# A two-layer decoder on one core: scores in halves of keys, scaling a step later, and a router with fewer steps in its context attention

## The chip, the core and the metric

The kernel runs on one core of a Trainium2 chip. A core has five engines that take their instructions from queues of their own: TensorE (PE in the profile, its weight loads apart as PEld), VectorE (DVE), ScalarE (ACT), GpSimd (POOL) and SyncE (SP, which here only starts DMAs). The metric is the device time of one execution in microseconds (us); where a time stands alone it is the median of several executions. All data are 32-bit floats.

## What is computed

The program is a decoder of two layers over 8 batches of 512 tokens with 256 features, with a context of 64 rows per batch. Each layer has a self-attention, an attention with the context and a feed-forward part, and a layer norm follows every part. The change touches the second layer's attention with the context and what prepares its experts. Of the reference these lines matter:

```python
def _L1_xattn_ref(x1, x2, Wq1, Wk1, Wv1, Wk2, Wv2, Wo, bo):
    ...
    q1 = split_heads(x1 @ Wq1, N1)
    k1 = split_heads(x1 @ Wk1, N1)
    v1 = split_heads(x1 @ Wv1, N1)
    k2 = split_heads(x2 @ Wk2, N2)
    v2 = split_heads(x2 @ Wv2, N2)
    k = jnp.concatenate([k1, k2], axis=1)
    v = jnp.concatenate([v1, v2], axis=1)
    sim = jnp.einsum('bihd,bjhd->bhij', q1.astype(jnp.float32), k.astype(jnp.float32)) * scale
    attn = jax.nn.softmax(sim, axis=-1)
    out = jnp.einsum('bhij,bjhd->bihd', attn, v)
    out = out.reshape(B, N1, h * d)
    return out @ Wo + bo

def _L1_ffn_ref(x, gamma, beta, router_w, W1, W2):
    ...
    xn = (x - mu) * jax.lax.rsqrt(var + EPS) * gamma + beta
    logits = jnp.einsum('btd,ed->bte', xn, router_w)
    probs = jax.nn.softmax(logits / TEMP, axis=-1)
    w, idx = jax.lax.top_k(probs, K)
    wdense = jnp.sum(jax.nn.one_hot(idx, E, dtype=w.dtype) * w[..., None], axis=-2)
    h = jax.nn.silu(jnp.einsum('btd,edf->betf', xn, W1))
    y = jnp.einsum('betf,efd->betd', h, W2)
    out = jnp.einsum('bte,betd->btd', wdense, y)
    return out + res
```

There are 8 heads of 64 and 8 experts. So a softmax runs over 576 keys (512 of the tokens, 64 of the context), and the experts' part needs, for every token, the two experts with the greatest weights. The kernel computes only those two: it sorts the tokens by expert in a table in memory.

## The kernel before

**Stages.** The program runs six stages one after the other: layer 0's self-attention, its context attention and feed-forward part, layer 1's self-attention, layer 1's context attention (about 2175 to 3031 us in the trace), the experts (to about 3558 us), and the last norm. The change lies in the fourth stage, with its ends reaching into the fifth.

**The pipeline of the context stage.** `_pipeline` (L32) walks over units and, in each step, calls a list of stages, each with a lag. The units are batch b (8), pair of heads c (4) and query tile i (4 tiles of 128 tokens): 128 steps. In each step stand, in this order (L1491 ff.): `l1x_scores` of this unit, `l1x_transposes` of the unit two steps ago, `l1x_values` of the unit six steps ago, and `l1x_ahead`. At the end of each step one piece of a list `put_off` is taken and run. In this stage PE executes strictly the written order (`tc.manual_schedule(engines={PE})`); the other engines' instructions are ordered by a scheduler when the program is built, except where `keep_in_program_order` stands.

- `l1x_scores`: for each of the two heads j, one matmul over the 512 token keys (L1100) and one over the 64 context keys (L1102) into a tile `s_sc` of two PSUM banks; then DVE takes the negated maximum `nm` (L1104), ACT the exponential with the sum beside it (L1105), and `scaled` (L898) the reciprocal of the sums (`rsum`, L900) and the scaling of p by it (L902). The context keys `k2` are computed once ahead of the stage. A head's 64 rows of q and k lie in partitions 0 to 63 or 64 to 127.
- `l1x_transposes`: one transposition of the middle 128 columns of p, which hold the context part of both heads (`tP2`, L1115), and four for each head (`tP`, L1120); each is copied out of PSUM by `evac` (L104), which gives every other copy to DVE (L108) and the rest to ACT (L110).
- `l1x_values`: o is summed over key tiles (L1132), and with the last tile the context's values are added (L1140). Then `out_done` (L961) follows: o is copied into `aT`, and after the fourth pair of heads the two halves of the output projection (`project_and_norm`, L239) are put on `put_off`. The second half ends in `normed`, the layer norm (DVE `bn_stats` and `bn_aggr`, POOL's power for the inverse root L216, DVE's x at L223).
- `l1x_ahead`: in step i=0 the q projection of the next pair of heads, in i=2 its k, in i=3 its v (L1057, L1067); k's result is copied to SBUF by DVE (L1062). In i=1 the transposition of the next batch's x (`tT`, L198) or its context values, in some pairs.

**Banks.** PSUM has two score tiles of two banks (s), three transposition tiles of one bank (t), and one o tile. With one o tile `u_tile` (L98) gives t tiles too, so the projections (`t_qk`, `t_v`), the output projection and the router all share the three t banks with `tP` and `tP2`.

**The router's pieces.** `routed` (L1472) puts behind each batch's output projection: nothing, `route_norm`, nothing, `route_transposes`, nothing, `route_picks`, nothing, `route_places`, one for each step. So one batch's router runs beside the next batch's attention. `route_norm` (L1180) makes z, a row tile with one buffer, and stores 2x as the start of the sum `total`. `route_transposes` turns z (`tZ`, L1198). `route_picks` (L1208) makes the logits (`o_r`, L1213), the softmax over 8 experts, the two picks, and writes weights and token numbers into z (L1243, L1244). `route_places` (L1247) counts with 14 small matmuls (`o_rank`, L1252 to L1256) how many tokens have taken each expert ahead of each token, works out the rows, and POOL scatters z's rows into the table `rows_in` with eight indirect DMAs (L1268). The first few lines of the counting:

```python
for i in range(NT):
    pe.matmul(o[:, i * NE : (i + 1) * NE], lhsT=under, rhs=both[:, i, :], start=True, stop=(i == 0))
    for j in range(i):
        pe.matmul(o[:, i * NE : (i + 1) * NE], lhsT=ones, rhs=both[:, j, :], start=False, stop=(j == i - 1))
```

**To the experts.** For batch 6, `routed` also puts `early_blocks` (which expert and which rows each of the first blocks of 256 rows takes) and the load of the first block on `put_off`. Batch 7's router pieces go on `last_route` and run beside the first blocks of the expert stage. A block goes through `moe_load` (L1383: SP loads the rows xr, then the two weights, `we`), a step with nothing, `moe_pre` (transposes, L1403), `moe_up` (L1425) and `moe_down` (L1433). `moe_down` computes both token tiles of a block in one bank `o_y` (L1442), DVE scales each (L1462), and POOL adds each to `total` with an indirect DMA (L1463). The last stage loads `total`, takes the norm and stores it.

Of the kernel before, what the change touches and what calls it, by code (L numbers as in the profile page):

```python
# [11 lines left out]
F32 = mybir.dt.float32  # L12
# [6 lines left out]
P = 128  # L19
# [30 lines left out]
def decoder_kernel(ctx: ExitStack, tc: tile.TileContext, a: dict, out: bass.AP):  # L50
# [967 lines left out]
    NC2 = NB * S2  # L1018
    k2 = slot("k2").rearrange("p (c n) -> p c n", c=4)
# [28 lines left out]
    def l1x_project(b, c, what):  # L1048

        xT = live["xT", b]  # L1050
        cols = slice(c * P, (c + 1) * P)
        if what == 0:
            live["qk", b, c] = qk_tiles()
        if what < 2:
            t = t_tile("t_qk").rearrange("p i n -> p (i n)")
            for kc in range(KC):
                pe.matmul(t, lhsT=(wq1, wk1)[what][:, kc, cols], rhs=xT[:, kc, :], start=(kc == 0), stop=(kc == KC - 1))  # L1057
            if what == 0:

                act.mul(live["qk", b, c][0], t, 0.125)  # L1060
            else:
                dve.tensor_copy(live["qk", b, c][1], t)  # L1062
            return
        t = t_tile("t_v")
        for j in range(NT):
            for kc in range(KC):
                pe.matmul(  # L1067
                    t[:, j, :],
                    lhsT=xT[:, kc, j * P : (j + 1) * P],
                    rhs=wv1[:, kc, cols],  # L1070
                    start=(kc == 0),
                    stop=(kc == KC - 1),
                )
        v = ph.tile([P, NT, P], F32, tag="vc", name="vc", bufs=3)
        act.copy(v, t)
        live["qkv", b, c] = *live.pop(("qk", b, c)), v
# [13 lines left out]
    def l1x_scores(b, c, i):  # L1090
        q, k, _ = live["qkv", b, c]
        p = p_tile(S + S2, bufs=4)
        sums = col("sums", 4)
        nm = col("nm", 2)
        for j in range(2):
            h = 64 * j
            lhsT = q[h : h + 64, i * P : (i + 1) * P]
            s = s_tile("s_sc").rearrange("p t n -> p (t n)")

            pe.matmul(s[:, S * j : S * (j + 1)], lhsT=lhsT, rhs=k[h : h + 64, :], start=True, stop=True)  # L1100
            at = S - S2 * j
            pe.matmul(s[:, at : at + S2], lhsT=lhsT, rhs=k2[h : h + 64, c, b * S2 : (b + 1) * S2], start=True, stop=True)  # L1102
            s = s[:, at * j : at * j + S + S2]
            dve.tensor_reduce(nm[:, j : j + 1], s, AX.X, ALU.max, negate=True)  # L1104
            act.activation(p[:, j, :], s, AF.Exp, bias=nm[:, j : j + 1], accum_out=sums[:, j : j + 1])  # L1105
        scaled(p, sums, S + S2)
        live["p", b, c, i] = p

    def l1x_transposes(b, c, i):
        p = live.pop(("p", b, c, i)).rearrange("p j n -> p (j n)")  # L1110
# [5 lines left out]
        evac(pt2[:, i * P : (i + 1) * P], t)  # L1116
        for j in range(2):
# [3 lines left out]
            evac(pt[j][:, :, i * P : (i + 1) * P], t)  # L1121
# [86 lines left out]
    def route_picks(b):  # L1208
# [11 lines left out]
        pr, top, hit, rest = e_tile("pr"), e_col("top"), e_tile("hit"), e_tile("rest")  # L1220
# [5 lines left out]
        dve.tensor_tensor(pr, pr, over_e(top), ALU.mult)  # L1226

        left = pr
        picks = []
        for k in range(2):  # L1230
            pick = e_tile(f"pick{k}")
            dve.tensor_reduce(top, left, AX.X, ALU.max)
            dve.tensor_tensor(hit, left, over_e(top), ALU.is_equal)
            dve.tensor_tensor(hit, hit, over_i(rev), ALU.mult)
            dve.tensor_reduce(top, hit, AX.X, ALU.max)
            dve.tensor_tensor(pick, over_i(rev), over_e(top), ALU.is_equal)
            if k == 0:
                dve.scalar_tensor_tensor(rest, pick, -2.0, pr, ALU.mult, ALU.add)
                left = rest
            picks.append(pick)  # L1240
        both, z = e_tile("both"), live["z", b]
# [3 lines left out]
        live["picks", b] = picks, both  # L1245

    def route_places(b):  # L1247

        picks, both = live.pop(("picks", b))
        o = u_tile("o_rank")  # L1250
        for i in range(NT):
            pe.matmul(o[:, i * NE : (i + 1) * NE], lhsT=under, rhs=both[:, i, :], start=True, stop=(i == 0))  # L1252
            for j in range(i):
                pe.matmul(o[:, i * NE : (i + 1) * NE], lhsT=ones, rhs=both[:, j, :], start=False, stop=(j == i - 1))
        for i in range(NT):
            pe.matmul(o[:, NT * NE : (NT + 1) * NE], lhsT=ones, rhs=both[:, i, :], start=(i == 0), stop=(i == NT - 1))  # L1256
# [178 lines left out]
    def moe_down(n):  # L1435
# [3 lines left out]
        o = u_tile("o_y").rearrange("p (i n) -> p i n", i=TILES)  # L1439
        for i in range(size):  # L1440
            for f in range(8):
                pe.matmul(  # L1442
                    o[:, i, :],
# [17 lines left out]
        for i in range(size):  # L1461
            dve.tensor_scalar(y[:, i, :], o[:, i, :], share[:, i : i + 1], None, ALU.mult)  # L1462
# [11 lines left out]
    def routed(b):  # L1474
        pieces = [partial(f, b) for f in (route_norm, route_transposes, route_picks, route_places)]
# [5 lines left out]
        for piece in pieces:  # L1481
            put_off.extend((nothing, piece))
# [4 lines left out]
    with phase("l1_context") as ph, tc.manual_schedule(engines={PE}):  # L1487
        l1x_share(0)
        l1x_context_values(0)
        for what in range(3):  # L1490
# [3 lines left out]
            [(0, l1x_scores), (2, l1x_transposes), (6, l1x_values), (0, l1x_ahead)],  # L1494
# [111 lines left out]
```

## Time and profile before

| | us |
|---|---|
| median of 3 runs (lowest, highest) | 3592.87 (3590.85, 3603.25) |
| the profiled execution: its time | 3602.03 |
| its span in the trace | 3600.3 |
| context stage of layer 1, 2175 to 3031: PE, DVE, ACT, POOL busy | 796.3, 537.0, 335.9, 83.4 of 856 |
| expert stage, 3031 to 3558: PE, DVE, ACT, POOL busy | 519.8, 67.0, 120.5, 117.0 of 527 |

The profile is one execution, recorded by the hardware; its granted TensorE clock was 0.961 over the span. In the listing of instructions each line has start, duration, engine, line of the kernel, operation, output and input by their names with partitions and columns (`64*128 64x512` is a weight of 64 rows and 128 columns against 64 rows and 512 columns), and how many of them are joined (`x4`; a matmul of 32-bit data shows as two, its two passes, and a transposition as one); in brackets the time that the engine stood idle before, and what released it. In the list of waits the numbers are total us, times, longest us; the first name waits, the second released it. In the table by stretch the columns are the length, busy us of PE, PEld, DVE, ACT and POOL with their instruction counts, the granted clock, the share of DMA and GB/s.

### The profile page before, as it was taken

The page shows a single profiled execution, that of the slowest core. Times are in us where ns is not written, and L with a number is a line of the kernel's source. Part 1 is how long each engine was busy: PE and PEld are TensorE (multiplying, and loading weights), DVE is VectorE, ACT ScalarE, POOL GpSimd, SP SyncE. Part 2 cuts the span into 40 slices and gives each one's busy share as a digit, 9 for nine tenths or more (in the row PEclk, how much of TensorE's full clock was granted, in tenths as well). Part 3 has the DMA queues.
Part 4 walks back from the last instruction along what each step waited for, and adds up shares of the span by engine and source line. Part 5 has one row for each costly group of instructions (what it writes and reads, how often), then busy time and mean ns, then how long its engine had stood idle before and what let it go on. Part 6 is the DMA issues. An engine that isn't in the chain of part 4 may idle for free. (4 is left out here: it accounts for less than half of the span.)

```text
span 3600.3 us, 52648 instructions
## 1 busy us (share of the span) xinstructions
PE 3374.1 (94%) x19718; PEld 2124.2 (59%) x19718; DVE 2080.9 (58%) x5710; ACT 1504.2 (42%) x3139; POOL 1097.2 (30%) x960
## 2 busy tenths in 40 slices
PE   8999999998999989999999999999999998999995
PEld 3333343345666656666666665555555555888884
DVE  5776766665666467777777766665666664201012
ACT  2444444443443345565555654433433333222222
POOL 3877777771111122222222210010110111222222
PEclk8999999997999999999999999999999998999997
DMA  4001011111000099332322320000000003666674
GB/s 133 31 16 32 18 34 38 34 46 32 5 2 1 1 233 255 42 42 36 40 38 36 42 42 4 10 19 16 19 14 14 19 13 125 207 189 184 185 230 133
DMA packets 166000, 234.96 MB, mean 65 GB/s; under 512 B 26569, under 2 KB 128649, under 8 KB 165746
## 3 DMA queue, kind: packets, MB, share of 16 engines
q1 hardware_dynamic: 139010, 175.83, 15.7%
q0 software_dynamic: 25584, 51.57, 9.6%
q8 instruction: 156, 2.56, 0.3%
q10 hardware_dynamic: 1152, 4.19, 0.3%
q14 instruction: 98, 0.80, 0.1%
HBM read 135.83 MB, written 61.11 MB: 55 GB/s over the span
## 5 line engine op out<-in xcount | busy, mean ns | idle before, releaser
L428 DVE CUSTOM_DVE_ANT_0 scored<-s_sc,decay 128x512 f32<-128x512 f32 x512 | 323.5, 687 | 220.5 <-PE s_sc L423 219.4
L281 ACT ACTIVATE p<-p,nm 128x128 f32<-128x128 f32 (+3 forms) x512 | 282.5, 553 | 301.3 <-DVE nm L270 300.0
L865 POOL DMA_DIRECT2D qk<-turned x256 | 207.9, 1228 | 592.5 <-issue 303.8
L481 ACT ACTIVATE pt<-s_st 128x1024 f32<-128x1024 f32 x256 | 261.1, 1023 | 272.0 <-PE s_st L477 240.3
L1105 ACT ACTIVATE p<-s_sc,nm 128x576 f32<-128x576 f32 x256 | 191.1, 747 | 342.5 <-DVE nm L1104 241.9
L902 DVE TENSOR_SCALAR p<-p,rsum 128x576 f32<-128x576 f32 (+4 forms) x768 | 300.1, 432 | 9.8
L1425 PE MATMUL s_h<-xnT,we 128*128 128x256 f32 (+1 forms) x1248 | 261.6, 363 | 1.5 <-DMA we<-in_mo_w 1.5
L1462 DVE TENSOR_SCALAR y<-o_y,share 128x256 f32<-128x256 f32 x71 | 31.4, 479 | 398.6 <-PE o_y L1442 398.6
L270 DVE CUSTOM_DVE_ANT_0 p<-s_sc,tabs 128x128 f32<-128x128 f32 (+3 forms) x512 | 225.1, 483 | 55.8 <-PE s_sc L925 55.7
L1442 PE MATMUL o_y<-we,h 128*128 128x256 f32 x1136 | 251.4, 379 | 0.0
L1104 DVE TENSOR_REDUCE nm<-s_sc 128x1 f32<-128x576 f32 x256 | 185.2, 748 | 114.1 <-PE s_sc L1102 112.7
L1425 PEld LDWEIGHTS s_h<-xnT,we 128*128 128x128 f32 x1248 | 217.5, 192 | 26.3 <-DMA we<-in_mo_w 1.9
L1442 PEld LDWEIGHTS o_y<-we,h 128*128 128x128 f32 x1136 | 215.3, 190 | 29.0
L1463 POOL DMA_INDIRECT total<-y,to x71 | 110.2, 1552 | 399.2 <-DVE y L1462 173.2
L423 PE MATMUL s_sc<-k,q 32*128 32x512 f32 x1024 | 175.2, 674 | 26.8 <-ACT pt L481 23.2
L958 ACT COPY pt<-tP 128x384 f32<-128x384 f32 (+1 forms) x384 | 172.9, 513 | 44.6 <-PE tP L957 44.1
L925 PE MATMUL s_sc<-qk 64*128 64x128 f32 (+3 forms) x1024 | 176.8, 460 | 12.8 <-DMA qk<-turned 9.1
L1268 POOL DMA_INDIRECT rows_in<-z,irow x64 | 62.8, 981 | 410.6 <-DVE hit L1263 304.3
L1120 PE MATMUL tP<-ident,p 128*128 128x128 f32 x1024 | 143.5, 282 | 40.4 <-DVE k L1062 25.1
L957 PE MATMUL tP<-ident,p 128*128 128x128 f32 x1280 | 169.4, 276 | 5.8 <-ACT pt L958 4.5
L957 PEld LDWEIGHTS tP<-ident,p 128*128 128x128 f32 x1280 | 144.7, 141 | 49.7 <-issue 28.0
L981 PE MATMUL o_pv<-pt,vc 128*64 128x128 f32 (+1 forms) x2304 | 167.5, 290 | 0.0
(282 smaller groups left out, 6632.6 us busy)
## 6 DMA issues: line engine op xcount, KB each, us to landing
we<-in_mo_w SPq DMA_DIRECT2D x78, 1024.0 KB, 6.0
rows_in<-zero SPq DMA_DIRECT2D x64, 530.0 KB, 13.2
qk<-turned POOLq DMA_DIRECT2D x256, 128.0 KB, 4.5
coef<-in_ff_upw SPq DMA_DIRECT2D x40, 256.0 KB, 3.0
coef<-in_ff_dnw SPq DMA_DIRECT2D x40, 256.0 KB, 3.1
xr<-rows_in SPq DMA_DIRECT2D x32, 265.0 KB, 6.4
x<-in_x SPq DMA_DIRECT2D x8, 512.0 KB, 10.0
total<-x SPq DMA_DIRECT2D x8, 512.0 KB, 2.9
```

The source lines that it names most:

```text
L270: dve.tensor_tensor_reduce(out=p[:, j, 0:n], in0=s[:, j, 0:n], in1=m, scale=-scale, scalar=3.0e38, op0=ALU.add, op1=ALU.min, accum_out=nm[ ...
L281: act.activation(p[:, j, 0:n], p[:, j, 0:n], AF.Exp, bias=nm[:, j : j + 1], scale=-1.0, accum_out=sums[:, at + j : at + j + 1],)
L428: dve.tensor_tensor_reduce(out=scored[:, h, :], in0=s[:, j, :], in1=decay[:, i, :], scale=1.0, scalar=-3.0e38, op0=ALU.mult, op1=ALU.max, ...
L481: act.activation(pt, s, AF.Exp, scale=1.0 / 16.0)
L865: pool.dma_start(out=qk[h : h + 32], in_=other[g : g + 32], accum_op=ALU.add)
L902: dve.tensor_scalar(p[:, j, 0:n], p[:, j, 0:n], rsum[:, j : j + 1], None, ALU.mult)
L925: pe.matmul(s[:, j, at : at + n], lhsT=q[h : h + 64, i * P : (i + 1) * P], rhs=k[h : h + 64, 0:n], start=True, stop=True,)
L957: pe.transpose(t[:, n, :], p[:, j, at * P : (at + 1) * P], ident)
L1104: dve.tensor_reduce(nm[:, j : j + 1], s, AX.X, ALU.max, negate=True)
L1105: act.activation(p[:, j, :], s, AF.Exp, bias=nm[:, j : j + 1], accum_out=sums[:, j : j + 1])
L1425: pe.matmul(s[:, j, :], lhsT=w1[:, c, f * P : (f + 1) * P], rhs=xnT[:, c, :], start=(c == 0), stop=(c == KC - 1),)
L1442: pe.matmul(o[:, i, :], lhsT=h[:, f, i * P : (i + 1) * P], rhs=w2[:, f, :], start=(f == 0), stop=(f == 7),)
```

## The change

- **Halves of keys.** The k tile of a pair of heads grows by 128 columns and holds the context keys too: behind the token keys for head 0 and ahead of them for head 1. POOL copies them there, two copies of 64 x 64 for each pair. The scores of a head are two matmuls over 288 columns each, one half in each of the tile's two banks, written alternately (half 0 of both heads, then half 1 of both). The maximum and the exponential read 2 x 288.
- **Order of a step.** `l1x_scores` holds only the matmuls; maximum and exponentials are a stage of their own, `l1x_probs`, listed behind the transposes; the scaling is another, `l1x_scaled`, with a lag of one step. The copies of the transposes have fixed engines: `tP2` and head 0's `tP` on ACT, head 1's `tP` on DVE.
- **Router.** `route_norm` is run in the same step as the second half of the output projection. `route_picks` is split in three pieces (`route_odds`, `route_pick`, `route_picks`). The row of pieces is product and norm, nothing, transposes, odds, pick, picks, places: eight steps with the first half of the product, where there were ten. For batch 7, the pieces are six instead of four, behind the same two steps of nothing.
- **Counting.** A fifth, zero tile is kept behind the four tiles of `both` (a POOL memset writes it), and five matmuls of 40, 32, 24, 16 and 8 columns take the place of the 14 of 8.
- **Experts.** `moe_down` uses one `o_y` bank for each token tile instead of one for both.

```diff
@@ l1x_project
         if what == 0:
-            live["qk", b, c] = qk_tiles()
+            q = ph.tile([P, S], F32, tag="q", name="q")
+            live["qk", b, c] = q, ph.tile([P, S + 2 * S2], F32, tag="k", name="k")
...
-                dve.tensor_copy(live["qk", b, c][1], t)
+                k = live["qk", b, c][1]
+                dve.tensor_copy(k[:, S2 : S2 + S], t)
+                for h, at in ((0, S2 + S), (64, 0)):
+                    pool.tensor_copy(k[h : h + 64, at : at + S2], k2[h : h + 64, c, b * S2 : (b + 1) * S2])
@@ l1x_scores
+        ss = [s_tile("s_sc")[:, :, 0:HALF] for _ in range(2)]
+        for t in range(2):
+            for j, s in enumerate(ss):
+                h = 64 * j
+                at = S2 * (1 - j) + HALF * t
+                pe.matmul(
+                    s[:, t, :], lhsT=q[h : h + 64, i * P : (i + 1) * P], rhs=k[h : h + 64, at : at + HALF], start=True, stop=True
+                )
+        live["s", b, c, i] = ss
+
+    def l1x_probs(b, c, i):
         p = p_tile(S + S2, bufs=4)
         sums = col("sums", 4)
         nm = col("nm", 2)
-        for j in range(2):
...
-            pe.matmul(s[:, S * j : S * (j + 1)], lhsT=lhsT, rhs=k[h : h + 64, :], start=True, stop=True)
-            at = S - S2 * j
-            pe.matmul(s[:, at : at + S2], lhsT=lhsT, rhs=k2[h : h + 64, c, b * S2 : (b + 1) * S2], start=True, stop=True)
-            s = s[:, at * j : at * j + S + S2]
-            dve.tensor_reduce(nm[:, j : j + 1], s, AX.X, ALU.max, negate=True)
-            act.activation(p[:, j, :], s, AF.Exp, bias=nm[:, j : j + 1], accum_out=sums[:, j : j + 1])
+        for j, s in enumerate(live.pop(("s", b, c, i))):
+            dve.tensor_reduce(nm[:, j : j + 1], s, AX.XY, ALU.max, negate=True)
+            act.activation(
+                p[:, j, :].rearrange("p (t n) -> p t n", t=2), s, AF.Exp, bias=nm[:, j : j + 1], accum_out=sums[:, j : j + 1]
+            )
+        live["p", b, c, i] = p, sums
+
+    def l1x_scaled(b, c, i):
+        p, sums = live["p", b, c, i]
         scaled(p, sums, S + S2)
-        live["p", b, c, i] = p
@@ l1x_transposes
-        evac(pt2[:, i * P : (i + 1) * P], t)
+        act.copy(pt2[:, i * P : (i + 1) * P], t)
...
-            evac(pt[j][:, :, i * P : (i + 1) * P], t)
+            (act.copy, dve.tensor_copy)[j](pt[j][:, :, i * P : (i + 1) * P], t)
@@ route_picks
+        picked = work.tile([P, NT + 1, NE], F32, tag="both", name="both", bufs=1)
+        pool.memset(picked[:, NT, :], 0.0)
+        both, z = picked[:, 0:NT, :], live["z", b]
@@ route_places
-        for i in range(NT):
-            pe.matmul(o[:, i * NE : (i + 1) * NE], lhsT=under, rhs=both[:, i, :], start=True, stop=(i == 0))
-            for j in range(i):
-                pe.matmul(o[:, i * NE : (i + 1) * NE], lhsT=ones, rhs=both[:, j, :], start=False, stop=(j == i - 1))
-        for i in range(NT):
-            pe.matmul(o[:, NT * NE : (NT + 1) * NE], lhsT=ones, rhs=both[:, i, :], start=(i == 0), stop=(i == NT - 1))
+        tiles = picked.rearrange("p i e -> p (i e)")
+        pe.matmul(o[:, 0 : (NT + 1) * NE], lhsT=under, rhs=tiles, start=True, stop=False)
+        for i in range(1, NT + 1):
+            n = (NT + 1 - i) * NE
+            pe.matmul(o[:, i * NE : (NT + 1) * NE], lhsT=ones, rhs=tiles[:, 0:n], start=False, stop=(i == NT))
@@ moe_down
-        o = u_tile("o_y").rearrange("p (i n) -> p i n", i=TILES)
-        for i in range(size):
+        os = [u_tile("o_y")[:, 0:D] for _ in range(size)]
+        for i, o in enumerate(os):
...
-            dve.tensor_scalar(y[:, i, :], o[:, i, :], share[:, i : i + 1], None, ALU.mult)
+            dve.tensor_scalar(y[:, i, :], os[i], share[:, i : i + 1], None, ALU.mult)
@@ routed
-        pieces = [partial(f, b) for f in (route_norm, route_transposes, route_picks, route_places)]
+        pieces = [partial(f, b) for f in (route_norm, route_transposes, route_odds, route_pick, route_picks, route_places)]
...
-        for piece in pieces:
-            put_off.extend((nothing, piece))
+        product = put_off.pop()
+        put_off.extend([lambda: (product(), pieces[0]()), nothing] + pieces[1:])
@@ the stages of the pipeline
-            [(0, l1x_scores), (2, l1x_transposes), (6, l1x_values), (0, l1x_ahead)],
+            [
+                (0, l1x_scores),
+                (2, l1x_transposes),
+                (0, l1x_probs),
+                (1, l1x_scaled),
+                (6, l1x_values),
+                (0, l1x_ahead),
+            ],
```

The three pieces of `route_picks` in the changed kernel hold the same instructions as before: `route_odds` the logits and the softmax, `route_pick` the first pick, `route_picks` the second one and the weights in z.

## Prediction on record

> **What bounds the kernel now.** I read the page first, then the busy time by stretch, then the list of waits of the context stage (2175 to 3031 us, lines 1018 to 1491), then the timeline of single steps in it, and last the two places where this stage's routing reaches further: the start of the expert stage and the end of the kernel. The page and the stretches:
>
> ```profile
> PE 3374.1 (94%) x19718; PEld 2124.2 (59%) x19718; DVE 2080.9 (58%) x5710; ACT 1504.2 (42%) x3139; POOL 1097.2 (30%) x960
> ...
> 2175.00:3031.00 856.00, 796.27 (x4267) 466.34 (x4265) 537.02 (x1325) 335.95 (x813) 83.36 (x76) 0.96 0.05 15
> ...
> 3027.20:3047.40 20.20, 11.48 (x41) 8.67 (x40) 8.08 (x35) 4.00 (x5) 3.01 (x3) 0.66 0.73 249
> ```
>
> PE is the bound: 796 of the stage's 856 us are matmul (columns after the length: PE, PEld, DVE, ACT, POOL busy, then granted clock). So I can win only PE work, PE waits (some 60 us) and granted clock (0.96, so 34 us lost at half clock). The second row is the seam to the experts: 20 us at clock 0.66. The waits of PE in the stage, with DVE's one on the scatters:
>
> ```profile
> PE tP L1120 <- DVE k L1062: 25.1, 6, 5.4
> PE tP L1120 <- DVE pt L108: 7.3, 6, 1.4
> PE tP L1120 <- ACT pt L110: 6.0, 6, 1.7
> PE t_qk L1057 <- ACT pt L110: 5.3, 9, 0.9
> PE t_qk L1057 <- DVE pt L108: 3.2, 5, 0.7
> DVE z L1244 <- DMA rows_in<-z,irow: 32.6, 6, 6.7
> ```
>
> The first and last belong together: once per batch DVE stands at L1244 until the previous batch's eight scatters have landed (z is one buffer), k's copy stands behind it, and PE has no free t bank. The next two are the norm region, where one norm follows another. PE's timeline of an ordinary step:
>
> ```profile
> 2237.09 1.14 PE L1100 MATMUL s_sc<-k,q 64*128 64x512 f32 x4
> 2238.05 0.34 PE L1102 MATMUL s_sc<-k,q 64*128 64x64 f32 x4
> 2238.33 0.33 PE L1115 MATMUL tP<-ident,p 128*128 128x128 f32 x1
> ...
> 2239.46 1.08 PE L1132 MATMUL o_pv<-pt,vc 128*64 128x512 f32 x4
> 2240.47 1.98 PE L1057 MATMUL t_qk<-xT,q_k 128*128 128x512 f32 x4
> 2242.38 1.14 PE L1100 MATMUL s_sc<-k,q 64*128 64x512 f32 x4
> ```
>
> From start to start: scores 1.24, transposes 1.13, values 1.01, next projection 1.91; 5.29 us a step. The seam and the end:
>
> ```profile
> 3020.25 7.17 PE L239 MATMUL o_out<-v_o,aT 128*128 128x256 f32 x32
> 3033.96 0.69 PE L1403 MATMUL tZ<-ident,xr 128*128 128x128 f32 x2 [6.54 <-DMA xr<-rows_in]
> 3035.31 0.69 PE L1403 MATMUL tZ<-ident,xr 128*128 128x128 f32 x2 [0.66 <-ACT xnT L1404]
> 3037.52 8.70 PE L1425 MATMUL s_h<-xnT,we 128*128 128x256 f32 x26 [1.52 <-DMA we<-in_mo_w]
> ...
> 3554.99 1.55 POOL L1463 DMA_INDIRECT total<-y,to  x1 [8.93 <-DVE y L1462]
> 3559.50 1.55 POOL L1463 DMA_INDIRECT total<-y,to  x1 [2.96 <-DMA total<-y,to]
> ```
>
> **The change, part by part.** All sums are made on the profiled execution (3602.0 us, span 3600.3, 1.7 around it), 9.2 above the median of 3592.9; I take differences from it and apply them to the median.
>
> *Halves of keys.* Four matmuls (two passes each) as before, 288 columns instead of 512 and 64. In the timeline both 512s share one start, so the two heads already run side by side: 1.24 us for 576 columns. A 512 pass is 427 ns (1.91 us for four, less 0.2), so 288 is 240: 4 passes 0.96, plus the 0.1 before and 0.17 after that the old row also holds (1.24 less 0.427x2 and 0.056x2, estimate). 1.23: nothing gained. [...] The trace decides: 1.24, so 0. The reduction and exponential over 2x288 have the nearest rows L1104 (748 ns) and L1105 (747) for the same 576 elements; between 0 and 0.1 us each, hidden by 2.2 us of DVE idle and 2 us of ACT idle in a 5.3 us step. The 64 x 64 key copies on POOL (two per head pair) are in no row: between 0.13 (a memset 128x8) and 0.73 us (L730, 128x256); I take 0.3. They are made 2.5 steps (13 us) ahead, except where scatters stand in POOL's queue (below).
>
> *Closer router.* o_rank: 28 passes took 3079.06 to 3082.10, 3.04 us; the new form has 10, at the same 0.11: 1.1. Saved 1.9 x 8 = 15 us, all on PE.
>
> *Copies ahead of exponentials.* tP2's copy always goes to ACT in front of the first exponential, so the t bank for the next projection is free about 1.9 us after the step begins and asked for at 3.4. The t_qk rows (8.5) and the tT row (ACT pt, 1.7) go outside of the norm region; I take 6. ACT then ends its exponentials at 4.3 us of a step; the shortest step (i=1, 4.38) still doesn't wait.
>
> *Scaling a step later.* DVE's waits on the accumulator (58.8 us at L900) go, but DVE isn't the bound. The price is slack: p is scaled at 4.4 us of the step before its transposes and needed at 4.38 + 1.24 = 5.6 in the shortest case, so 1.2 us are left where there were 5. Ordinary steps stay free. In the norm region DVE now has both norms in one row: after pt come x (4 x 0.32), four bn_stats and aggregations (1.7), and only then the scaling that PE needs next; with POOL's power in between (1.5 us from ve to x), I work out 26.6 us for the scaling against 24.2 for PE, and a late nm for the step after: 2.4 + 1.3 = 3.7 us per batch. Before, the same place cost 3.0 (tP start to values 2327.29 to 2331.43 is 4.14 against 1.13, less half of clock loss gives 2.2, plus smaller waits of 2): 4.3. So -0.6 x 7 = -4.
>
> *The stall at L1244.* It stays. In the changed order the copy of token numbers again stands four steps behind the ranks. From the end of o_rank: indices at 1.0, first scatter 1.45, the eighth landed 22.9 later (2467.49 to 2490.33) at 24.4, the scaling behind it done at 25.9; PE wants it at 21.5. The POOL queue adds one thing: the key copies for the next batch stand between scatter 5 and scatter 6, and the second waits for scatter 5 to land, at 16.2, while those scores are due at 15.0: 1.5 us, which come off the later wait. Sum 4.4 us a batch against 4.1 before (25.1 / 6): +0.4 x 6 = +2. What is queued behind the DVE wait is the scaling, and PE's transposes wait for that.
>
> *Seam to the experts.* For batch 6 places come two steps earlier (8 instead of 10 pieces): 4.4 + 3.4 us of attention now lie between its ranks and PE's end, so o_out ends about 31.7 us after o_rank where it was 24 (3003.2 to 3027.2). Scatters land at 24.4, rows and weights 6.5 later (3031.1 to 3037.5) at 31: hidden. On SP, the next block's load no longer stands behind `total<-x` (3039.5), so its weights come in time. The 20.2 us from 3027.2 to the second block's first matmul become tZ and s_h at full clock, 1.6 + 6.8 + 0.5: 8.9. Saved 11 us.
>
> *o_y in two banks.* PE's order is unchanged. At the end the first half of the last pair is out 3.5 us earlier, and with it the whole row of `total<-y` adds: -3.5.
>
> *Picks in two pieces* move small DVE work (12 of about 0.15) to other steps: 0. A later late_blocks (by two steps of 14 us) has slack of a dozen steps: 0.
>
> *Clock.* The gaps of 4.1 to 5.4 us were mostly followed by half clock: 0.72 from 2486 to 2498 and 0.75 even after the 2.1 us pair at 2327. [...] By the rows a pair of 2.1 us is enough in half of the cases; I keep 24 of 34: -10.
>
> Sum: -15 -6 -4 +2 -11 -3.5 -10 = -47.5; I round to -45, as the small parts overlap. 3592.9 - 45 = 3548.
>
> **The rivals.**
> (1) The sum above: 3548, own range 3535 to 3562. Chance 0.45.
> (2) [...] the norm waits shrink as well, DVE having no accumulator waits: -45 -24 = 3524. Against it: the 0.75 and 0.76 stretches after short gaps. 0.2.
> (3) The seam doesn't close: a load of the second block waits for memory of the context stage, and PE's idle only moves one block on. For it: xr of that block waits for PE, ACT and DVE in the changed order. -45 +11 = 3559. 0.13.
> (4) DVE's lateness eats most: norm region 8 instead of 3.7 us a batch, with clock behind it: +30, 3578. 0.12.
> (5) Slower: scaling late makes DVE the releaser of every transpose. PE then waits x in each of 128 steps; it decides from x = 45/128 = 0.35 us, which takes nm and scaling 1.2 + 0.35 us longer than their rows, for instance by slow reductions across two banks. At x = 0.5: +64 - 45, 3612. Against it: DVE is busy 4.2 of 6.7 us a step. 0.05.
> (6) Halves do bring the heads side by side[...]: -45 - 88 = 3460. Against it: the shared start. 0.05.
>
> **How the numbers follow.** A measurement of this kernel tells about 0.5% (18 us) from no change, so faster means below 3575. Faster: (1), (2), (3), (6): 0.83. Same: (4), 0.12. Slower: (5), 0.05. The range from 3520 to 3579 takes in (1) to (4) and leaves out (5) and (6) and a part of (2).
>
> **What would show it.** Right: L1103 with both heads' passes at one start and about 1.23 us to the next transpose; o_rank about 1.1 us; t_qk waits gone; a wait of DVE on the scatters of about 5 us per batch still there, with PE's tP behind DVE p; PE's s_h starting within 2 us of o_out; three `total<-y` adds 3.5 us earlier. Wrong: a step that waits for DVE p at each transpose (rival 5), scores well below 1.2 us (6), s_h gaps of several us in the second block (3), or no wait on the scatters at all.

## The result and the profile after

The changed kernel takes 3563.21 us (median of 5 runs, 3553.12 to 3571.18) against 3593.02 (5 runs, 3590.85 to 3603.25): the medians are 29.8 us apart, and the ratio over all runs is 0.9906 (interval 0.9885 to 0.9927), or some 34 us faster. 3548 was forecast, 45 us faster. The profiled execution took 3557.96 us, span 3555.9, 44.4 less than the one of before. The stretches show which part of that belongs to the change:

| stretch (us) | before | after | difference |
|---|---|---|---|
| start to the first scores of the context stage | 2177.75 | 2167.08 | -10.7 |
| from there to the end of the last `o_out` ("the stage") | 849.67 | 829.94 | -19.7 |
| from there to the last matmul | 530.22 | 519.76 | -10.5 |
| from there to the end | 42.66 | 39.12 | -3.5 |

The change does not touch the code of the first stretch. Its length lies between 2164 and 2184 us in the twelve kernels below too, and half clock loses 68 to 87 us there. So single executions differ by up to 20 us for a reason that no edit here reaches, and I compare stages, not spans. Each kernel's stage is read from one execution, so a difference of a few us in it is one sample; the medians stand beside it. The change is worth -33.7 us in the other three. Here are the page and the two rows by stretch that answer to those of before (context stage, then experts up to the last matmul):

```profile
PE 3355.1 (94%) x19574; PEld 2105.9 (59%) x19574; DVE 2068.8 (58%) x5646; ACT 1525.0 (43%) x3203; POOL 1115.2 (31%) x1032
...
2167.08:2997.02 829.94, 788.77 (x4125) 455.74 (x4124) 522.60 (x1257) 356.62 (x877) 100.31 (x143) 0.94 0.05 18
2997.02:3516.78 519.76, 514.44 (x2561) 448.96 (x2558) 70.65 (x354) 120.57 (x155) 118.44 (x80) 1.00 0.66 193
```

The stage's granted clock has fallen, from 0.96 to 0.94, while that of the experts is full. The main wait of PE in the stage and two of DVE's:

```profile
PE s_sc L1103 <- ACT p L1114: 38.3, 22, 5.2
...
DVE rsum L900 <- ACT p L1114: 84.4, 92, 1.5
...
DVE z L1267 <- DMA rows_in<-z,irow: 46.6, 7, 8.7
```

The two that answer to the first two of them in the kernel before:

```profile
PE s_sc L1100 <- ACT p L1105: 2.4, 3, 1.5
DVE rsum L900 <- ACT p L1105: 58.8, 101, 1.1
```

Of the eleven kinds of waits that PE had before, one is left that matters, and it was small there: the scores wait until an exponential has read their tile (2.4 us before, 38.3 now). DVE's wait for the exponentials has grown. The scores of an ordinary step with the transposes behind them, the seam, and two of the last adds to `total`:

```profile
2339.31 1.24 PE L1103 MATMUL s_sc<-k,q 64*128 64x288 f32 x8
2340.48 0.33 PE L1129 MATMUL tP<-ident,p 128*128 128x128 f32 x1
...
2989.85 7.17 PE L239 MATMUL o_out<-v_o,aT 128*128 128x256 f32 x32
2996.86 0.38 PE L1426 MATMUL tZ<-ident,xr 128*128 128x128 f32 x2
...
3510.68 1.55 POOL L1486 DMA_INDIRECT total<-y,to  x1 [5.48 <-DVE y L1485]
3515.02 1.55 POOL L1486 DMA_INDIRECT total<-y,to  x1 [2.79 <-DMA total<-y,to]
```

The scores take 1.17 us from start to start instead of 1.24 (1.233 to 1.171 in the medians of all steps). PE goes on to the experts without a wait; one of 0.7 us and one of 2.4 follow in the first blocks.

**Where the stage loses time now.** Each batch has two places. At the norm (A), DVE's timeline, then PE's:

```profile
2297.53 1.39 DVE L223 TENSOR_SCALAR z<-x,mv,rs 128x256 f32<-128x256 f32 x4 [0.90 <-POOL rs L216]
...
2299.43 0.69 DVE L1202 TENSOR_SCALAR x<-x 128x1024 f32<-128x1024 f32 x1
2300.03 1.42 DVE L1113 TENSOR_REDUCE nm<-s_sc 128x1 f32<-128x576 f32 x2
...
2301.76 3.50 PE L1103 MATMUL s_sc<-k,q 64*128 64x288 f32 x8 [1.54 <-ACT p L1114]
```

The maxima of scores that were ready at 2294.2 come at 2300.0, behind z and the doubling of x; the exponential follows, and PE waits 1.54 us. Behind the scatters (B), the maxima stand behind the copy of the token numbers:

```profile
2354.67 0.17 DVE L1267 COPY z<-tokens_at 128x4 f32<-128x4 f32 x1 [6.78 <-DMA rows_in<-z,irow]
...
2357.54 3.49 PE L1103 MATMUL s_sc<-k,q 64*128 64x288 f32 x8 [3.32 <-ACT p L1114]
```

And behind both, the clock. The third column from the end is the granted clock, for the stretch behind A, the 44 us between, and the stretch behind B:

```profile
2301.76:2309.07 7.31, 7.19 (x22) 3.55 (x22) 3.91 (x8) 4.71 (x11) 0.00 (x0) 0.53 0.11 39
2309.07:2353.14 44.07, 44.07 (x260) 25.83 (x258) 27.43 (x71) 20.14 (x50) 9.06 (x13) 1.00 0.07 22
...
2357.54:2363.07 5.53, 5.53 (x17) 3.44 (x17) 3.34 (x7) 2.75 (x8) 0.00 (x0) 0.50 0.01 3
```

Scores that take 1.24 us take 3.5 there. At half clock the eight transposes behind them (L1134) take 1.91 us, where those of the ordinary step take 1.04 (at 2340.65); and the second head's passes, which start at 2302.97, also wait inside that row for their own exponential (ACT, L1114, 2302.09 to 2302.83). The windows of half clock last 3.41, 6.83 or 10.24 us: 12 in the stage in the trace of before, 32.4 us lost; 14 after, all but the first behind A or B, 46.1 lost (half of the time at half clock).

**Theory.** The change removes work and waits as forecast, but leaves two waits a batch, and each costs itself and then a window of half clock, 3.2 us lost at A and 3.7 at B in the mean. **Rivals.** Half clock follows the load and not the waits; the waits at B are late scatters, which would only move; the halves or the copies ahead cost time by themselves.

### The profile page after: what moved, and what is told of

Same layout as the page of the kernel before. It is cut to its first block, busy times and chain, and to the rows that moved or that the text cites. A ratio compares the mean times of both kernels' runs of the same rounds, so it can differ in the third digit from the quotient of the medians.

```text
span 3555.9 us, 52606 instructions
## 1 busy us (share of the span) xinstructions
PE 3355.1 (94%) x19574; PEld 2105.9 (59%) x19574; DVE 2068.8 (58%) x5646; ACT 1525.0 (43%) x3203; POOL 1115.2 (31%) x1032
## 3 DMA queue, kind: packets, MB, share of 16 engines
q10 hardware_dynamic: 1152, 4.19, 0.3%
## 5 line engine op out<-in xcount | busy, mean ns | idle before, releaser
L270 DVE CUSTOM_DVE_ANT_0 p<-s_sc,tabs 128x128 f32<-128x128 f32 (+3 forms) x512 | 225.1, 483 | 56.8 <-PE s_sc L925 56.7
L1114 ACT ACTIVATE p<-s_sc,nm 128x576 f32<-128x576 f32 x256 | 191.4, 748 | 116.4 <-DVE nm L1113 110.5
L1448 PEld LDWEIGHTS s_h<-xnT,we 128*128 128x128 f32 x1248 | 215.4, 190 | 23.9 <-ACT xnT L1427 0.2
L1103 PE MATMUL s_sc<-k,q 64*128 64x288 f32 x1024 | 190.1, 457 | 38.4 <-ACT p L1114 38.3
L957 PE MATMUL tP<-ident,p 128*128 128x128 f32 x1280 | 169.4, 276 | 5.9 <-ACT pt L958 4.6
L1103 PEld LDWEIGHTS s_sc<-k,q 64*128 64x128 f32 x1024 | 102.6, 197 | 119.9 <-ACT p L1114 61.9
```

The costliest lines, as they stand in the source:

```text
L270: dve.tensor_tensor_reduce(out=p[:, j, 0:n], in0=s[:, j, 0:n], in1=m, scale=-scale, scalar=3.0e38, op0=ALU.add, op1=ALU.min, accum_out=nm[ ...
L957: pe.transpose(t[:, n, :], p[:, j, at * P : (at + 1) * P], ident)
L1103: pe.matmul(s[:, t, :], lhsT=q[h : h + 64, i * P : (i + 1) * P], rhs=k[h : h + 64, at : at + HALF], start=True, stop=True)
L1114: act.activation(p[:, j, :].rearrange("p (t n) -> p t n", t=2), s, AF.Exp, bias=nm[:, j : j + 1], accum_out=sums[:, j : j + 1])
L1448: pe.matmul(s[:, j, :], lhsT=w1[:, c, f * P : (f + 1) * P], rhs=xnT[:, c, :], start=(c == 0), stop=(c == KC - 1),)
```

## The experiments

All of them in one table (the ratios below are to executions of the kernel before in the same runs, whose medians lay between 3591 and 3597): waits are PE's idle stretches of over 0.15 us in the stage; lost clock is half of the stage's time at half clock. "a" is made from the changed kernel, "b" from the kernel before, "both" from the first run of that name.

| kernel | median | stage | waits | lost clock | `o_out` to last matmul |
|---|---|---|---|---|---|
| before | 3593.0 | 849.7 | 54.7 | 32.4 | 530.2 |
| after | 3563.2 | 829.9 | 41.1 | 46.1 | 519.8 |
| a_token_in_place | 3522.1 | 785.7 | 19.8 | 22.2 | 519.1 |
| b_token_in_place | 3564.2 | 810.1 | 29.4 | 15.4 | 532.6 |
| a_z_behind_nm | 3528.1 | 795.4 | 32.0 | 20.5 | 517.5 |
| a_512_and_64 | 3548.0 | 805.3 | 25.7 | 17.1 | 523.1 |
| both_waits_gone | 3485.9 | 753.6 | 10.0 | 3.4 | 519.8 |
| both_gone_512_and_64 | 3499.6 | 765.6 | 7.9 | 6.8 | 520.5 |
| a_scaled_same_step | 3561.7 | 835.7 | 46.3 | 47.8 | 522.2 |
| a_copies_not_ahead | 3553.4 | 816.5 | 49.5 | 29.0 | 520.4 |
| b_router_pieces | 3565.4 | 820.1 | 34.3 | 22.2 | 522.0 |
| b_count_and_banks | 3577.1 | 831.0 | 56.8 | 23.9 | 531.8 |
| both_gone_copies_late | 3485.5 | 755.4 | 12.7 | 1.7 | 522.8 |
| both_gone_scaled_same | 3497.1 | 761.9 | 16.1 | 5.1 | 523.8 |

### The wait behind the scatters

```diff
-        dve.tensor_copy(z[:, :, D + NE], tokens_at[:, b * NT : (b + 1) * NT])
+        tc.keep_in_program_order(dve.tensor_copy(z[:, :, D + NE], tokens_at[:, b * NT : (b + 1) * NT]))
```

This copy depends on nothing but the buffer z, and the scheduler has moved it far ahead: in the trace after it runs at 2354.7, where its batch's picks are written into z at 2427.8, 73 us later. In its written place it comes behind the picks, when the scatters have long landed. Only this instruction changes its place.

> The changed kernel, with one edit: the copy of the token numbers into z (L1267) is kept in its written place, behind the picks, instead of 40 instructions of VectorE earlier. Theory (each PE wait of about 1.5 us or more costs itself and then a window of half clock): the six waits of the scores behind this copy (3.3, 3.0, 3.8, 5.2, 2.8 and 3.3 us in the profile, 21.5 in sum) and the windows behind them (44.4 us, half of it lost, 22) go: some 43 us, 3520. Rival 1 (half clock follows the load, not the waits): only the 21.5 go, 3541, and the trace still shows about 14 windows in the stage. Rival 2 (the waits come from late scatters and return elsewhere, at the norm that writes z): nothing gained, 3563.

Measured: 3522.08, ratio to before 0.9796 (0.9771 to 0.9821). The stage is 44.3 shorter: waits -21.3, clock -23.9, and 8 windows are left of 14. So it is as the theory has it, and both rivals fall. What is left of the scores' waits is mostly A:

```profile
PE s_sc L1103 <- ACT p L1114: 17.0, 17, 1.5
```

> The kernel before, with the same one edit (L1244). Theory: the 25.1 us of waits behind k's copy go and the windows behind five of them (27.3 us, 13.7 lost): 39 us, 3554. Rival 1: 25, 3568. Rival 2: nothing, 3593. If both this and the other kernel gain what the theory says, the change is worth some 34 us without the stall as with it.

Measured: 3564.24, ratio 0.9909 (0.9889 to 0.9929). The stage is 39.6 shorter, what the theory gave; 2.4 come back at the seam, where PE, now earlier, waits 8.5 us for the rows. The median fell by 32 us only, 10 short of the theory: the profiled execution of the kernel before, from which the 39.6 is taken, was one of its slower ones. Rival 2 falls: the waits did not move. Rival 1 falls for the five windows behind the six waits, which are gone with them; but behind `o_rank` there are now five windows instead of three (see `b_router_pieces`). This one edit is worth as much to the kernel before as the whole change.

### The wait at the norm

```diff
-        normed(z[:, :, 0:D], xs[b])
-        dve.tensor_scalar(xs[b], xs[b], 2.0, None, ALU.mult)
+        live["z", b], live["mv", b] = z, moments(xs[b])
...
-        put_off.extend([lambda: (product(), pieces[0]()), nothing] + pieces[1:])
+        put_off.extend([lambda: (product(), pieces[0]()), nothing, lambda: (route_z(b), pieces[1]())] + pieces[2:])
```

`moments` is the first half of `normed`, `route_z` writes z, doubles x and stores it. DVE takes both maxima ahead of z.

> The changed kernel, with the second norm split: its moments stay where they were, and the writing of z and the doubling of x run two steps later, with the transposes of z, so that VectorE takes the maxima of that step first. Theory: the wait of the scores for the exponential behind each norm (1.53 us and 0.27 at the transposes, seven times) becomes several of 0.2 to 0.7 us at the transposes of z, 0.9 in sum, too short for a window: 7 x 0.9 = 6 and 7 windows (44 us, 22 lost), 28 in all: 3535. Rival 1 (half clock follows the load): -6, 3557. Rival 3: the transposes of z now wait 1.5 us in one piece, and wait and window stay: 3563.

Measured: 3528.13, ratio 0.982 (0.9796 to 0.9843); the stage is 34.5 shorter: waits -9.1, clock -25.6. The waits (the transposes of z stand at L1227 there):

```profile
PE s_sc L1103 <- ACT p L1114: 26.4, 14, 4.4
PE tZ L1227 <- ACT p L1114: 4.7, 7, 0.8
```

A wait of 0.75 us at the transposes is followed by no window. Rivals 1 and 3 fall.

> The changed kernel with both edits of the first runs together: the token copy kept in its written place, and the writing of z behind the maxima two steps later. Theory: the two waits are apart in time (55 us), so their gains add: 3563 - 41 - 35 = 3487, and in the stage only the windows at its two ends are left. Rival (the clock gives some half time in any case, and only moves it): about 3500 or more, with windows at places without a wait ahead of them.

Measured: 3485.92, ratio to before 0.9702 (0.9672 to 0.9731), faster than both kernels: by 105 us than the one before in the same runs (3591.07), by some 77 than the changed one. The stage at clock 1.00:

```profile
2173.44:2927.01 753.57, 743.59 (x4125) 433.16 (x4124) 520.03 (x1257) 359.15 (x877) 100.52 (x143) 1.00 0.06 20
```

The same matmuls as in the changed kernel (x4125) take 743.6 us instead of 788.8. The gains add: 44.3 + 34.5 = 78.8, and 76.4 were measured. Two windows are left, at the two ends of the stage; the rival falls.

### The parts of the change

Halves undone (in `l1x_scores`; the order of the four matmuls is then that of before, and POOL copies no keys):

```diff
-                pe.matmul(
-                    s[:, t, :], lhsT=q[h : h + 64, i * P : (i + 1) * P], rhs=k[h : h + 64, at : at + HALF], start=True, stop=True
-                )
+            pe.matmul(s[:, S * j : S * (j + 1)], lhsT=lhsT, rhs=k[h : h + 64, :], start=True, stop=True)
+            at = S - S2 * j
+            pe.matmul(s[:, at : at + S2], lhsT=lhsT, rhs=k2[h : h + 64, c, b * S2 : (b + 1) * S2], start=True, stop=True)
```

> The changed kernel with the halves of keys undone: per head a matmul over 512 token keys and one over 64 context keys, no copies of context keys. Theory: the scores of a step go back from 1.171 us (start to start, after) to 1.233 (before), 128 x 0.062 = 8 us: 3571, and the six late scatters behind the key copies come 0.8 us earlier, which gives back up to 5: 3566 to 3571. Rival (the halves bring nothing by themselves, the shorter step comes of the order in which the four are written): scores 1.17, 3563 or less.

Measured: 3547.99, ratio 0.9869 (0.9847 to 0.9892): 15 us faster than the changed kernel, against theory and rival, although the scores take 1.233 us again; the stage is 24.6 shorter. The place is A. DVE, then PE:

```profile
2309.41 0.75 DVE L1110 TENSOR_REDUCE nm<-s_sc 128x1 f32<-128x576 f32 x1
2310.69 1.38 DVE L223 TENSOR_SCALAR z<-x,mv,rs 128x256 f32<-128x256 f32 x4 [0.53 <-POOL rs L216]
...
2313.18 0.75 DVE L1110 TENSOR_REDUCE nm<-s_sc 128x1 f32<-128x576 f32 x1
...
2313.32 1.12 PE L1099 MATMUL s_sc<-k,q 64*128 64x512 f32 x2
...
2314.86 1.12 PE L1099 MATMUL s_sc<-k,q 64*128 64x512 f32 x2 [0.25 <-ACT p L1111]
```

Here head 0's scores are complete before head 1's begin in the written order, and the scheduler placed head 0's maximum ahead of z. PE then starts head 0 on time and spends the wait for head 1 on its matmuls: idle 0.25 us, not 1.5, and no window at any norm. With the four halves written alternately both maxima land behind z. That the order of writing and not the halving moved the maximum is my reading; no run changed the order alone. The six waits at B are shorter too, 17.0 us against 21.5: without POOL's copies of keys the sixth scatter follows the fifth after 2.9 us in the median, not 3.4.

> The same as the run both_waits_gone, with the halves of keys undone (512 and 64 columns per head again). In the changed kernel this undoing gained 15 us although the scores of a step took 1.233 instead of 1.171 us, since VectorE's order in the norm came out otherwise. Theory: with the waits gone on both sides only the 0.062 us is left, 128 x 0.062 = 8 us slower than both_waits_gone: 3495. Rival (the halves cost something else too, such as a start that needs both score tiles free at once): equal or faster, 3487 or less.

Measured: 3499.61, ratio 0.974 (0.9712 to 0.9769). The stage is 12.0 longer, of it 3.4 clock: 8.6, near the theory's 8, and the rival falls. So the halves are worth some 8 us, and in the changed kernel they cost more than that through an order that they brought about.

Scaling back in its step, and copies behind the exponentials:

```diff
-                (1, l1x_scaled),
+                (0, l1x_scaled),
```

```diff
-                (2, l1x_transposes),
                 (0, l1x_probs),
+                (2, l1x_transposes),
...
-            (act.copy, dve.tensor_copy)[j](pt[j][:, :, i * P : (i + 1) * P], t)
+            evac(pt[j][:, :, i * P : (i + 1) * P], t)
```

> The changed kernel with the scaling put back into the step of its exponentials (lag 0). Theory: the lag moved nothing in an ordinary step, since the scheduler puts the reciprocal and the scaling behind the same step's exponentials in either case (VectorE's waits there, 84.4 us at L900, are longer than before, not gone): 3563, within 5, and the same waits. Rival (the lag is what takes VectorE's slack at the norms): the waits of the scores shrink, 3545. Rival (the lag helps): 3575.

Measured: 3561.67, ratio 0.9915 (0.9885 to 0.9944); the stage is 5.8 longer in an execution that was the slowest of six, and DVE's wait at L900 is 84.3 us, as with the lag (84.4). The median is the theory's; both rivals fall.

> The run both_waits_gone with the scaling in the step of its exponentials. Theory: the same order of work in ordinary steps, the stage 754 within 2, 3486. Rival: the lag is needed where VectorE is late, so waits of the transposes for the scaled p return at the norms: 3495.

Measured: 3497.05, ratio 0.9731 (0.9707 to 0.9756); the stage is 8.3 longer. My theory falls: at the norms the lag does move something. Without it the transposes of z wait 6.0 us more, for z, which now comes behind the scaling:

```profile
PE tZ L1227 <- DVE z L1217: 6.0, 7, 0.9
```

The rival named the right place and some of the size, but not the instruction that waits.

> The changed kernel with the copies of the transposes behind the exponentials again and given to VectorE and ScalarE in turn. Theory: the waits for a bank at the projections come back (9 to 11 us in the profile of before, 0 after), the two big waits of each batch stay: 3572. Rival (copies ahead of the exponentials make these late, and that is what the scores wait for): 3550.

Measured: 3553.38, ratio 0.9885 (0.9855 to 0.9914); the waits are 8.4 longer, the clock loses 17.1 less, the stage is 13.5 shorter. The bank waits at the q and k projections do not come back, so the theory falls; the rival's number came near. At the norm PE waits once at the transposes of z, 2.2 to 2.8 us, in five batches, four of them with a window behind; in the other two it waits 1.0 and 1.5 us five us apart, with none.

> The run both_waits_gone with the copies of the transposes behind the exponentials again, given to VectorE and ScalarE in turn. There the two big waits do not hide what this part is worth. Theory: the bank waits that it removes are small (about 2 us at the projections of v and 2 at the transposes in the run a_copies_not_ahead) and no window hangs on them: the stage 754 + 4 = 758, 3490. Rival (the prediction's own term): the waits at the projections come back, 754 + 8 = 762 and a few windows, 3495 to 3500. Rival (copies ahead cost time, as the 13 us of the run a_copies_not_ahead seem to say): 745, 3477.

Measured: 3485.47, ratio 0.9699 (0.9677 to 0.972); the stage is 1.8 longer, and the median is that of both_waits_gone (3485.92). The theory's 4 us is near; neither rival came. So the copies ahead are worth 2 us at most, and the 13.5 of the run before came of the large waits: 17.1 less clock against 8.4 more waits, and 4.8 that neither column holds.

Last, two parts alone on the kernel before: the router's pieces, and counting with the two banks. Their edits are those of the diff above.

> The kernel before with the router's pieces of the changed kernel alone (norm with the product, picks in three pieces, eight steps instead of ten; the counting with 14 matmuls stays). Theory: the seam to the experts closes (20.2 us from the end of o_out to the second block's matmul become some 9, the whole from there to the last matmul 530 becomes 520), since the ranks of batch 6 come two steps earlier; the stall behind the token copy stays; at the norm z and the doubling of x stand ahead of a maximum here too, one of the two: -10, 3581. Rival 1 (the seam closed because of the other order on SyncE, or of the shorter stage): 3591, and the seam stays near 20. Rival 2 (the closer norm brings the wait of 1.5 us and seven windows with it): +20 in the stage, 3601.

Measured: 3565.37, ratio 0.9923 (0.9899 to 0.9947). The seam closes (530.2 to 522.0), so rival 1 falls. The stage is 29.6 shorter, where the theory had its 10 us at the seam alone and rival 2 a loss: the waits behind k's copy and at the norm, 38.4 us, become 14.5 at the scores and 14.6 at the transposes of z; those of the q and k projections for a bank, 8.5, become 0.8 (of the v projection 2.3 instead of 0.6). Three windows stand behind no wait at all. One of them, with `o_rank` in the first row and what follows in the second:

```profile
2548.89:2552.34 3.45, 3.45 (x30) 3.42 (x28) 0.15 (x1) 0.60 (x1) 0.00 (x0) 0.89 0.00 0
2552.34:2558.58 6.24, 6.24 (x23) 3.28 (x22) 4.44 (x15) 2.20 (x6) 2.00 (x2) 0.51 0.12 43
```

PE is busy all the time, with 28 passes of 8 columns. What in the pieces shortened the waits of PE I did not separate.

> The kernel before with the counting in five matmuls and the two o_y banks alone. Theory: o_rank 1.1 instead of 3.04 us, seven times in the stage (13.5) and once behind it (1.9); the last adds to the sum 3.5 us earlier: 19, 3572, the stage 836, the end 39.1 after the last matmul. Rival (PE wins nothing, since the stall behind the token copy then begins as much earlier and is as much longer): -5, 3586, with waits behind k's copy of 25 + 13 us.

Measured: 3577.13, ratio 0.9954 (0.9936 to 0.9973). The stage is 18.6 shorter, not 13.5: the clock loses 8.5 less, and no window stands behind `o_rank` any more. The end is 39.29 us, as after. k's waits are not longer by 13 us:

```profile
PE tP L1120 <- DVE k L1062: 26.6, 6, 5.4
```

The rival falls. At the seam PE, being earlier, waits 8.1 us for the rows, so nothing is won there, and the whole is 18 us by the medians where 19 were forecast.

## Why the prediction was right, and where it was not

The direction, the counting and the end were right, and the seam nearly so; the total was 11 us too hopeful. That it was not further off is partly luck: the clock came out 24 us worse than forecast, and waits and halves 14 us better. Its terms against the profile:

| term | forecast | measured |
|---|---|---|
| counting, eight times | -15 | -15.4 (3.04 to 1.11 us) |
| waits: projections, norm, stall | -6 -4 +2 | -13.6 |
| halves | 0 | -8 |
| clock | -10 | +13.7 in the stage |
| seam, without the counting there | -11 | -8.6 |
| two banks at the end | -3.5 | -3.5 |
| sum | -47.5 | -35.4 (the stretches: -33.7) |

**The step that failed is the clock:** "By the rows a pair of 2.1 us is enough in half of the cases; I keep 24 of 34". The forecast counted gaps by size and expected fewer half-clock windows from smaller gaps. In the changed kernel all 13 of the waits at A and B have a window behind them, the seven of 0.27 and 1.53 us too; at A the window (mostly 6.8 us, 3.4 lost) costs more than the wait, at B about as much (22.2 us lost against 21.5). In the kernel before, pairs of 2.1 to 2.5 us at the norm have a window in 3 of 6 cases, as the prediction read it; here are the rows of the first of them:

```profile
2329.06 0.66 PE L1120 MATMUL tP<-ident,p 128*128 128x128 f32 x4 [1.44 <-DVE pt L108]
2330.39 1.12 PE L1120 MATMUL tP<-ident,p 128*128 128x128 f32 x4 [0.68 <-ACT pt L110]
```

The shorter pair at A has one in 7 of 7. So the size of a gap does not tell what follows it, and the forecast's step from smaller gaps to fewer windows does not hold (the counts are in the last section). The run without these waits loses 3.4 us in the stage. Rival 2 had the other 24 of the 34 us of lost clock back as well; at A the trace shows 0.53 behind 1.54 us, so it falls, and its total of 3524 was not reached either.

**The stall and the norm: right place, wrong waiter.** I let PE's transposes wait for the scaling. They don't: the scores wait, since their tile is free only when the exponential has read it, and the maximum for that exponential is what stands late on DVE. The cost of the stall was near (21.5 us of waits in six batches, 3.6 each, against 4.4); the wait for POOL's key copies, for which I had 1.5 us, does not show, and the copies put some 0.5 us between two scatters. The difference of the stall to before was summed wrongly: 25.1 / 6 is 4.2, so 4.4 gives +0.2 a batch, or +1 and not +2. That one instruction's place could remove the stall did not occur to me; it was worth 44 us.

**The scaling.** "DVE's waits on the accumulator (58.8 us at L900) go" was wrong: they grew to 84.4. I read the lag in the list of stages as an order on DVE, where the scheduler decides. It is the copies ahead of the exponentials that made them grow: with these undone they are 51.1 us (a_copies_not_ahead) and 55.6 (both_gone_copies_late), with the lag undone 84.3. With the large waits gone the lag is worth some 8 us, at the norms, a gain where I saw a price; in the changed kernel the median shows none.

**The copies ahead.** The bank waits at the projections (8.5 us) went, but in the run with the router's pieces alone they are 0.8, so the copies were not needed for it. What in the pieces removed them I did not test.

**The halves.** The heads' passes start in pairs before and after (13 and 7 ns apart in the median), so the row was right. Rival 6, whose 88 us were to come from bringing the heads side by side, fell. The size was off: beside the four passes, at 240 ns by my estimate, 0.21 us are left of a step's 1.17, where I had put 0.27 (in the medians the pairs start 340, 236 and 236 ns apart, the transposes 340 behind); 0.062 us in 128 steps is 8 us. That undoing the halves puts one maximum ahead of z, and so takes seven windows away, stood in no step.

**Rivals 3, 4 and 5.** The seam closes with a rest: one wait of 2.4 us for the rows of the third block. DVE is late at the norm, but PE waits 1.8 us a batch there and not 8; with the clock behind it, it is 4.9 (34.5 us in seven batches). In ordinary steps nothing waits for the scaled p.

So the whole is less than its parts: on the kernel before, the router's pieces alone take 29.6 us off the stage and the counting 18.6; with the halves' 8 that is 56, and the change got 19.7. By the whole times (ratios 0.9923 and 0.9954, and the 8) it is 52 against 34. The wait at A, which comes of both maxima behind z and cost 34.5 us, is in none of the parts alone and would fill the gap in the stage; that nothing else does is not shown.

## What to carry to other kernels

Count what PE waits for not in us of wait but in places: at A and B each wait cost itself and then 3.2 and 3.7 us of clock, so removing one wait in each batch wholly was worth more than shortening all. Do not read from the length of a wait whether half clock follows; look up the granted clock behind it (0.53 behind 1.54 us after, 1.00 behind 3.05 us before). Where a scheduler orders an engine, look at the order it built, above all for an instruction with few dependencies that it has moved ahead of its use and that waits for a buffer there; keeping one copy in its written place was worth 44 us here, more than a change in ten places. And judge the parts of a change with the large stalls gone, since beside them a part shows what it does to the stalls, not what it is worth.

## What the runs showed of the hardware

**Half clock did not follow the length of a wait.** Behind 0.27 and 1.53 us within 3 us of each other stood a window in 21 of 21 cases (after, a_token_in_place, a_scaled_same_step). Behind one wait of 2.2 to 2.8 us it was 4 in 5 (a_copies_not_ahead), behind one of 2.1 to 2.3 us 2 in 5 (b_router_pieces), behind 0.75 us none in 12 (a_z_behind_nm, both_waits_gone), behind two of 0.75 and 0.85 us 2 in 6 (both_gone_scaled_same). One wait of 3.05 us (before) had none: the clock is 1.00 from 2386.08 to 2393.00.

**Nor did PE's busy time ahead of it decide alone.** In the 3.41 us (as long as the shortest window) ahead of each of the 13 windows at A and B (after) PE is busy 0.9 to 2.2 us. In the two stretches of 3.41 us over the wait of 3.05 us (before, 2381.07 to 2384.48 and on to 2387.89) it is busy 1.96 and 1.81, at clock 1.00 and with no window behind.

**Behind narrow matmuls half clock came without a long wait.** Behind the 28 passes of 8 columns (3.04 us, PE busy, at most 0.6 us of wait ahead) stood 11 windows in 21 cases (before, b_token_in_place, b_router_pieces); behind the 10 passes of 8 to 40 columns (1.1 us) none in 14 (after, b_count_and_banks). Ahead of one of the 11 (before, 2353.76 to 2357.17) PE is busy for all of the 3.41 us. So the rival that half clock follows the load and not the waits was half right: the windows at A and B went with the waits, and those behind the 28 passes stand where PE hardly waits. What decides in general, these runs do not show.

**The passes of the two heads' scores start in pairs** whether 512 and 64 columns alternate or two times 288: 13 ns apart (before, L1100) and 7 ns (after, L1103) in the median. A step's scores, 1152 columns of two passes each, take 1.233 and 1.171 us. With 512 and 64, in the step at 2237.09 (before), all four passes of the two 512s start ahead of the 64s, although the first head's 64 are written before the second head's 512.
